# Softmax over the nodes of a graph in a two-layer graph network: from PE transposes for two graphs at a time to a DRAM round trip for one graph at a time

## The chip, the cores and the metric

The kernel runs on one core of a Trainium2 chip. The metric is the device time of one execution in microseconds; lower is better. The time before is 2011.91 us, the median of three runs (2011.75 to 2013.03).

## The reference, cut to what matters

There are 64 graphs (B) of 256 nodes (N) with 512 features (F), all in float32. The node mask is all ones. Two layers follow each other, each with a residual and a layer norm:

```python
# layer 0
deg = sum(adj, -1)
agg = (adj @ x) / max(deg, 1e-6)
x1  = layernorm(x + relu(concat([x, agg]) @ W.T))
# layer 1
q, k = split(x1 @ Wqk); v = x1 @ Wv
agg  = adj @ (k * mask)
w    = mask * sum(q * agg, -1) / sqrt(512)        # one score per node
out  = layernorm(x1 + softmax(w, over the 256 nodes)[:, None] * v)
```

What matters here is the softmax: each graph has 256 scores, one per node, and the softmax runs over all 256. In the kernel a graph's nodes lie on the 128 partitions in two halves, so the scores of one graph are a [128, 2] tile, and the maximum and the sum have to be taken across partitions.

## The kernel before, in words

One loop over i, from 0 to B + G + 1 with G = 2, runs a software pipeline over the graphs. In iteration i the program issues the loads of graph i + 2 (`load`, L78), the dense products of layer 0 for graph i (`layer0_a` L191, `layer0_b` L208), the row sums and the dense products of layer 1 for graph i - 2 (`turn` L286, `layer1_steps` L289), and the product of the adjacency with the values of graph i together with the x1 values of graph i - 1 (`gather_a` L222). After these come the combination and layer norm of layer 0 for graph i (`combine0` L269, `norm0` L277), which ends with the transposition of x1 by VectorE blocks and 16 small DMAs (`transpose_rows` L148, L157), and the degrees and sums for the next graph (`prepare` L173). Layer 1's q and k projections are merged into one matrix ahead of the loop (L110 to L116), so that the score of a node is the dot product of one row with its aggregated row; `dot` (L299) does that on VectorE as the products come out of PSUM.

Every matrix product is done in 2 x 2 blocks with seven block products instead of eight. A bank `u` collects several of them in turn: a product is added to it, ScalarE copies the partial result away (L197, L200, L204, L212 in layer 0; L304, L311, L318 in layer 1; L249, L255, L258, L262 in the gather), and the next product is added on top. TensorE therefore cannot add the next product on `u` before ScalarE's copy of the last is done; products on other banks (p2, p5) lie in between. All dense products are issued at L142, those of the gather at L240. PSUM has eight banks: seven are rotated by `bank()`, one (`ps_tp`) serves the transposes of the softmax.

The softmax works on two graphs at a time. `softmax_rows` (L328) takes the [128, 2, 2] scores of a pair, adds the partial dot and scales by the mask (L330, L331), and transposes them on TensorE (L335) so that each graph is one partition with 256 scores in PSUM. VectorE takes the maximum (L337, L338), ScalarE the exponential with its sum (L341), VectorE divides (L342, L343). `softmax_cols` (L346) transposes the result back on TensorE (L349) and copies it to SBUF (L351). `finish` (L353) multiplies v by the probabilities, adds x1 (L357), normalises (`layer_norm`, L160 to L171, with a square root at L167) and stores the output (L360). The pair's softmax is in the iteration in which i - 4 is even, and a graph is finished four iterations after its layer 0.

The program's text gives the order of dependencies and of priority; the order on each engine is laid out by the framework's planner, which fills all five engines' queues. Each engine then runs its queue strictly in order. SyncE (SP) issues all DMAs of the loop from one queue, so a DMA that waits for its data or buffer holds up those behind it.

Of the kernel before, what the change touches and what calls it, by code (L numbers as in the profile page):

```python
# [31 lines left out]
F32 = mybir.dt.float32  # L35
AF = mybir.ActivationFunctionType
OP = mybir.AluOpType
AX = mybir.AxisListType

P = 128  # L40
Q = 32
G = 2
DEG_EPS = 1e-6
LN_EPS = 1e-5

# [2 lines left out]
def resnorm_kernel(  # L48
# [12 lines left out]
    nc = tc.nc  # L61
    B, N, F = x.shape
    A = wqk_t.shape[0] // 2
    NT, NF, NA = N // P, F // P, A // P
    H, HF = NF // 2, F // 2
    assert NT == 2 and NF == 4
    inv_scale = 1.0 / float(A) ** 0.5

    const = ctx.enter_context(tc.tile_pool(name="const", bufs=1))
    pool = ctx.enter_context(tc.tile_pool(name="pool", bufs=2))  # L70
    small = ctx.enter_context(tc.tile_pool(name="small", bufs=4))
    ps_mm = ctx.enter_context(tc.tile_pool(name="ps_mm", bufs=7, space=bass.MemoryType.PSUM))
    ps_tp = ctx.enter_context(tc.tile_pool(name="ps_tp", bufs=1, space=bass.MemoryType.PSUM))

    (xs, adjs, rows, xTs, sums0, sumsA, rdegs, vals, owns, x1s, x1Ts, sums1, aggs, vs, scores, probs,
     open0) = ({} for _ in range(17))

    def load(g):  # L78
        xTs[g] = pool.tile([P, NF, N], F32, name="xT")
# [12 lines left out]
    with setup as sp:  # L92
# [8 lines left out]
        mask_sb = const.tile([P, NT, B], F32, name="mask_sb")  # L101
# [3 lines left out]
        ident = const.tile([P, P], F32, name="ident")  # L105
# [4 lines left out]
        ps = [ps_mm.tile([P, F], F32, name="mm") for _ in range(NF)]  # L110
# [6 lines left out]
    late = ctx.enter_context(tc.tile_pool(name="late", bufs=2))  # L117
# [22 lines left out]
    def product(ps, a, b, start=True):  # L140
        for c in range(H):
            nc.tensor.matmul(ps, a[:, c, :], b[:, c, :], start=start and c == 0, stop=(c == H - 1),  # L142
                             skip_group_check=True)

    def bank():
        return ps_mm.tile([P, F], F32, name="mm")

    def transpose_rows(src, dst):  # L148


        sq = pool.tile([P, P // Q, NF, NT, Q], F32, name="sq", bufs=1)
        for t in range(NT):
            nc.vector.transpose(sq[:, :, :, t, :].rearrange("p b c q -> p c b q"), src[:, t, :])
        to = dst.rearrange("f c (t a q) -> f (c t) a q", t=NT, q=Q)
        for a in range(P // Q):
            for b in range(P // Q):
                nc.sync.dma_start(to[b * Q:(b + 1) * Q, :, a, :],  # L157
                                  sq[a * Q:(a + 1) * Q, b].rearrange("p c t q -> p (c t) q"))

    def layer_norm(src, dst):  # L160
        mv = small.tile([P, NT, 2], F32, name="mv")
        for t in range(NT):
            st = small.tile([P, 6], F32, name="st")
            nc.vector.bn_stats(st, src[:, t, :])  # L164
            nc.vector.bn_aggr(mv[:, t, :], st)
        rstd = small.tile([P, NT], F32, name="rstd")
        nc.scalar.activation(rstd, mv[:, :, 1], AF.Sqrt, bias=eps)  # L167
        nc.vector.reciprocal(rstd, rstd)
        for t in range(NT):
            nc.vector.tensor_scalar(dst[:, t, :], src[:, t, :], mv[:, t, 0:1], rstd[:, t:t + 1],  # L170
                                    op0=OP.subtract, op1=OP.mult)  # L171
# [44 lines left out]
    def values(g):  # L216

        if g not in vals:
            vals[g] = pool.tile([P, 2, NT, F], F32, name="vals")
        return vals[g]  # L220
# [54 lines left out]
                                           op0=OP.max, op1=OP.add)  # L275

    def norm0(g):  # L277
        x1s[g] = pool.tile([P, NT, F], F32, name="x1", bufs=G + 4)
        layer_norm(owns.pop(g), x1s[g])
        for t in range(NT):  # L280
            nc.scalar.activation(values(g + 1)[:, 1, t, :], x1s[g][:, t, :], AF.Copy,  # L281
                                 scale=mask_sb[:, t, g:g + 1])
        x1Ts[g] = pool.tile([P, NF, N], F32, name="x1T")
        transpose_rows(x1s[g], x1Ts[g])

    def turn(g):  # L286
        sums1[g] = row_sums(x1Ts.pop(g), nc.vector)

    def layer1_steps(g):  # L289
        if g % G == 0:  # L290
            scores[g // G] = (small.tile([P, NT, G], F32, name="scores", bufs=2),
                              small.tile([P, G], F32, name="part", bufs=2))
        sc, part = scores[g // G]
        at = g % G
        s, w, agg = sums1.pop(g), W1, aggs.pop(g + 1)[:, 1]
        v = vs[g] = late.tile([P, NT, F], F32, name="v", bufs=G + 2)
        q = pool.tile([P, F], F32, name="q")

        def dot(a, t, to):  # L299
            nc.vector.scalar_tensor_tensor(q, a, 1.0, agg[:, t, :], op0=OP.mult, op1=OP.mult, accum_out=to)  # L300

        u = bank()
        product(u, s["A11"], w["B11"])
        nc.scalar.copy(q, u)  # L304
        dot(q, 0, part[:, at:at + 1])
        yield
        p5 = bank()
        product(p5, s["S1"], w["T1"])
        yield
        product(u, s["S2"], w["T2"], start=False)  # L310
        nc.scalar.copy(v[:, 0, :], u)  # L311
        yield
        p2 = bank()
        product(p2, s["A12"], w["B21"])
        dot(p2, 0, sc[:, 0, at:at + 1])
        yield
        product(u, s["S3"], w["T3"], start=False)
        nc.scalar.copy(v[:, 1, :], u)  # L318
        nc.vector.tensor_add(v[:, 1, :], p5, v[:, 1, :])  # L319
        yield  # L320
        product(u, s["A22"], w["T4"], start=False)
        dot(u, 1, sc[:, 1, at:at + 1])
        yield
        product(p5, s["S4"], w["B22"], start=False)
        nc.vector.tensor_add(v[:, 0, :], p5, v[:, 0, :])  # L325
        yield

    def softmax_rows(k):  # L328
        w, part = scores.pop(k)
        nc.vector.tensor_add(w[:, 0, :], w[:, 0, :], part)  # L330
        nc.vector.scalar_tensor_tensor(w, w, inv_scale, mask_sb[:, :, k * G:(k + 1) * G],  # L331
                                       op0=OP.mult, op1=OP.mult)
        wr = ps_tp.tile([G, NT, P], F32, name="tp")
        for t in range(NT):
            nc.tensor.transpose(wr[:, t, :], w[:, t, :], ident)  # L335
        top = small.tile([G, 1], F32, name="top")
        nc.vector.reduce_max(top, wr.rearrange("g t p -> g (t p)"), axis=AX.X)  # L337
        nc.vector.tensor_scalar(top, top, -1.0, None, op0=OP.mult)  # L338
        e = small.tile([G, NT, P], F32, name="e", bufs=2)
        total = small.tile([G, 1], F32, name="total")  # L340
        nc.scalar.activation(e, wr, AF.Exp, bias=top, accum_out=total)  # L341
        nc.vector.reciprocal(total, total)  # L342
        nc.vector.tensor_scalar(e, e, total, None, op0=OP.mult)  # L343
        return e

    def softmax_cols(k, e):  # L346
        ps = ps_tp.tile([P, NT, G], F32, name="tp")
        for t in range(NT):
            nc.tensor.transpose(ps[:, t, :], e[:, t, :], ident[:G, :G])  # L349
        probs[k] = small.tile([P, NT, G], F32, name="probs", bufs=2)  # L350
        nc.vector.tensor_copy(probs[k], ps)  # L351

    def finish(g):  # L353
        x1, v, p = x1s.pop(g), vs.pop(g), probs[g // G]
        o = pool.tile([P, NT, F], F32, name="o")
        for t in range(NT):
            nc.vector.scalar_tensor_tensor(o[:, t, :], v[:, t, :], p[:, t, g % G:g % G + 1], x1[:, t, :],  # L357
                                           op0=OP.mult, op1=OP.add)
        layer_norm(o, o)
        nc.sync.dma_start(out[g].rearrange("(t p) f -> p t f", p=P), o)  # L360
# [5 lines left out]
    def step(gen, n=1):  # L366
        for _ in range(n):
            next(gen, None)

    for i in range(B + G + 2):  # L370
        new = i < B
        if i + 2 < B:
            load(i + 2)
        k, at = divmod(i - G - 2, G)
        e = None
        if new:
            layer0_a(i)
        if at == 0 and 0 <= k < B // G:
            e = softmax_rows(k)
        if 0 <= i - 2 < B:  # L380
            turn(i - 2)
        l1 = layer1_steps(i - 2) if 0 <= i - 2 < B else iter(())
        step(l1)
        if new:
            layer0_b(i)
        if e is not None:
            softmax_cols(k, e)
        if 0 <= i - 2 - G < B:
            finish(i - 2 - G)
        z = gather_a(i) if i <= B else iter(())  # L390
        step(l1, 2)
        step(z)
        step(l1)
        step(z)
        step(l1)
        step(z)
        step(l1)
        step(z)
        step(l1)
        step(z)  # L400
        if new:
            combine0(i)
            norm0(i)
        if i + 1 < B:
            prepare(i + 1)
# [26 lines left out]
```

## Time and profile before

| what | value |
|---|---|
| median of three runs | 2011.91 us |
| the profiled execution, its own time | 2011.95 us |
| its span, first to last instruction | 2010.2 us |
| mean granted TensorE clock | 0.994 |
| ScalarE table loads | 32 at L341 (exponential), 33 at L167 (square root), 1 at L177, 1.283 us each |
| transposes on TensorE | 64 at L335 (0.273 us each), 64 at L349 (0.208 us mean) |
| largest single waits of TensorE | 6.2 us for the first weights, 4.1 us for a transposed x1 near the end |
| SyncE: time to landing, medians | x1T 2.0, adj 2.6, rows 2.6, out 3.1, x 3.5, xT 4.1 us |

The profile comes from one execution. Busy time of an engine is the union of the times of its instructions; TensorE's matmuls are pipelined, so the duration of one (0.59 us for 128x512) is longer than the step from one to the next (0.43 us). Each float32 matmul of the listing is two records. Line numbers such as L142 are lines of the kernel's listing; SPq is the queue of SyncE, PEld the weight loads of TensorE. The idle time in a line is the time in which the engine stood still before the instruction, with what ended it.

### The profile page before, as it was taken

The numbers are of one execution on the slowest core, as the hardware profiler recorded it, in microseconds if no ns is written. First come the engines' busy times: TensorE is split into PE (matmuls) and PEld (weight loads), VectorE is DVE, ScalarE is ACT, GpSimd is POOL, SyncE is SP. The second block draws the span as 40 slices with busy tenths as digits, with TensorE's granted clock in tenths as the row PEclk, the third lists the DMA queues.
The fourth block names the chain that finished last, engine by engine and source line by source line (L and its number), as shares of the span: only waits on it lengthen the run. The fifth ranks groups of instructions, "written<-read, shape, count | busy, mean of one in ns | idle before, by whom it ended". The sixth has DMA issues, their size and how long they took to land.

```text
span 2010.2 us, 19340 instructions
## 1 busy us (share of the span) xinstructions
PE 1973.9 (98%) x5536; PEld 1030.4 (51%) x5536; DVE 1523.6 (76%) x3184; ACT 673.2 (33%) x1354; POOL 419.0 (21%) x518
## 2 busy tenths in 40 slices
PE   7999999999999999999999999999999999999995
PEld 3555555555555555555555555555555555555552
DVE  3677787777787777787777887777877777877776
ACT  2333333333333332333332333333333333333322
POOL 4121221221221222212212212212212212222100
PEclk9999999999999999999999999999999999999998
DMA  7333333333333333323333333333333333233211
GB/s 241 85 71 94 88 79 94 86 82 91 88 81 92 90 80 84 99 77 86 90 87 86 80 94 89 79 94 85 81 92 90 81 91 86 68 79 79 62 38 53
DMA packets 384872, 174.40 MB, mean 87 GB/s; under 512 B 283776, under 2 KB 349440, under 8 KB 384768
## 3 DMA queue, kind: packets, MB, share of 16 engines
q1 hardware_dynamic: 382624, 168.97, 32.0%
q10 hardware_dynamic: 2144, 4.19, 0.6%
q8 instruction: 46, 0.75, 0.2%
q14 instruction: 58, 0.48, 0.1%
HBM read 105.97 MB, written 33.55 MB: 69 GB/s over the span
## 4 chain that ended last, share of the span: by engine, by line
PE 95%; DVE 1%; ACT 1%; SPq 0%; issue 0%; DMA 0%; DVEq 0%; ACTq 0%
PE mm L142 75%; PE mm L240 19%; SPq L157 0%; PE tp L349 0%; PE tp L335 0%; DVE st L164 0%; DVE o L357 0%; DVE own L272 0%; ACT L341 0%; ACT vals L281 0%; DMA x1T<-sq 0%; ACT rows L177 0%; DVE o L170 0%; DVE own L274 0%; DVE v L325 0%
## 5 line engine op out<-in xcount | busy, mean ns | idle before, releaser
L142 PE MATMUL mm<-w,s 128*128 128x512 f32 x1024 | 481.3, 592 | 0.7 <-ACT v L311 0.7
L142 PE MATMUL mm<-t,s 128*128 128x512 f32 x1024 | 466.2, 597 | 4.8 <-ACT own L197 3.8
L142 PEld LDWEIGHTS mm<-t,s 128*128 128x128 f32 x1024 | 192.3, 190 | 236.7 <-issue 215.5
L142 PEld LDWEIGHTS mm<-w,s 128*128 128x128 f32 x1024 | 194.4, 190 | 192.8 <-issue 163.2
L142 PE MATMUL mm<-w,x1T 128*128 128x512 f32 x512 | 242.5, 596 | 4.1 <-DMA x1T<-sq 4.1
L142 PE MATMUL mm<-w,xT 128*128 128x512 f32 x512 | 242.0, 594 | 0.0
L183 POOL TENSOR_TENSOR sa<-adj 128x128 f32<-128x128 f32 x64 | 47.1, 736 | 781.0 <-PE mm L240 774.3
L134 POOL TENSOR_TENSOR s<-xT 128x256 f32<-128x256 f32 x64 | 47.7, 745 | 703.6 <-PE mm L142 685.8
L240 PE MATMUL mm<-tv,sa 128*128 128x256 f32 x768 | 187.1, 379 | 0.0
L240 PEld LDWEIGHTS mm<-tv,sa 128*128 128x128 f32 x768 | 145.8, 190 | 74.6 <-issue 59.6
L142 PEld LDWEIGHTS mm<-w,xT 128*128 128x128 f32 x512 | 97.9, 191 | 95.8 <-issue 92.4
L272 DVE SCALAR_TENSOR_TENSOR own<-zr,rdeg,own 128x512 f32<-128x512 f32 x128 | 107.6, 841 | 44.4 <-ACT zr L262 44.4
L319 DVE TENSOR_TENSOR v<-mm,v 128x512 f32<-128x512 f32 x64 | 44.3, 692 | 126.3 <-ACT v L318 126.3
L142 PEld LDWEIGHTS mm<-w,x1T 128*128 128x128 f32 x512 | 95.3, 191 | 86.1 <-issue 74.6
L300 DVE SCALAR_TENSOR_TENSOR q<-mm,zr 128x512 f32<-128x512 f32 x128 | 87.7, 685 | 66.1 <-PE mm L142 66.1
L311 ACT COPY v<-mm 128x512 f32<-128x512 f32 x64 | 37.4, 585 | 299.0 <-PE mm L142 299.0
L142 PE MATMUL mm<-t,x1T 128*128 128x512 f32 x256 | 125.5, 612 | 0.7 <-ACT v L318 0.7
L142 PE MATMUL mm<-t,xT 128*128 128x512 f32 x256 | 120.6, 593 | 3.0 <-ACT vals L204 3.0
L240 PE MATMUL mm<-vals,adj 128*128 128x256 f32 x512 | 121.3, 379 | 1.6 <-DVE vals L214 1.6
L357 DVE SCALAR_TENSOR_TENSOR o<-v,probs,x 128x512 f32<-128x512 f32 x128 | 120.3, 959 | 0.1
L240 PEld LDWEIGHTS mm<-vals,adj 128*128 128x128 f32 x512 | 97.1, 190 | 43.2 <-issue 21.5
L214 DVE TENSOR_TENSOR vals<-mm,vals 128x512 f32<-128x512 f32 x64 | 44.3, 692 | 91.8 <-PE mm L142 91.8
(83 smaller groups left out, 2668.6 us busy)
## 6 DMA issues: line engine op xcount, KB each, us to landing
xT<-x_t SPq DMA_DIRECT2D x64, 512.0 KB, 4.1
x<-x SPq DMA_DIRECT2D x64, 512.0 KB, 3.5
x1T<-sq SPq DMA_DIRECT2D x1024, 32.0 KB, 2.0
out<-o SPq DMA_DIRECT2D x64, 512.0 KB, 3.1
adj<-adj_t SPq DMA_DIRECT2D x64, 256.0 KB, 2.6
rows<-adj SPq DMA_DIRECT2D x64, 256.0 KB, 2.6
wqk<-wqk_t ACTq DMA_DIRECT2D x4, 512.0 KB, 8.6
w<-w_t ACTq DMA_DIRECT2D x2, 1024.0 KB, 11.7
```

Source lines behind the costliest of these rows:

```text
L134: eng.tensor_add(s1, a21, a22)
L142: nc.tensor.matmul(ps, a[:, c, :], b[:, c, :], start=start and c == 0, stop=(c == H - 1), skip_group_check=True)
L183: nc.gpsimd.tensor_add(sa[:, 0], a21, a22)
L214: nc.vector.tensor_add(y[:, 0, :], p5, y[:, 0, :])
L240: nc.tensor.matmul(ps[:, k * HF:(k + 1) * HF], sumsA[g - k][a], w[b][:, n, :], start=start and n == 0, stop=True, skip_group_check=True)
L272: nc.vector.scalar_tensor_tensor(own[:, t, :], z[:, t, :], rdeg[:, t:t + 1], own[:, t, :], op0=OP.mult, op1=OP.add)
L300: nc.vector.scalar_tensor_tensor(q, a, 1.0, agg[:, t, :], op0=OP.mult, op1=OP.mult, accum_out=to)
L311: nc.scalar.copy(v[:, 0, :], u)
L319: nc.vector.tensor_add(v[:, 1, :], p5, v[:, 1, :])
L357: nc.vector.scalar_tensor_tensor(o[:, t, :], v[:, t, :], p[:, t, g % G:g % G + 1], x1[:, t, :], op0=OP.mult, op1=OP.add)
```

## The change

The softmax takes one graph at a time and no longer uses TensorE. `spread` scales the scores as before, stores the [128, 2] tile to a small DRAM tile as a row of 256, and reads this row back so that every partition holds all 256 scores. `softmax` then takes the negated maximum on VectorE and the exponential with its sum on ScalarE on all partitions alike, so that maximum and sum are at once where they are needed; a second exponential makes the graph's own [128, 2] probabilities from the scores still in SBUF. A graph is finished three iterations after its layer 0. `spread` stands at the head of the iteration behind the loads, `softmax` and `finish` in its middle. The bank of the transposes goes to the rotation (eight instead of seven), x1 has five buffers instead of six and v three instead of four.

```diff
-G = 2
...
-    ps_mm = ctx.enter_context(tc.tile_pool(name="ps_mm", bufs=7, space=bass.MemoryType.PSUM))
-    ps_tp = ctx.enter_context(tc.tile_pool(name="ps_tp", bufs=1, space=bass.MemoryType.PSUM))
+    ps_mm = ctx.enter_context(tc.tile_pool(name="ps_mm", bufs=8, space=bass.MemoryType.PSUM))
+    dram = ctx.enter_context(tc.tile_pool(name="dram", bufs=2, space=bass.MemoryType.DRAM))
...
-        x1s[g] = pool.tile([P, NT, F], F32, name="x1", bufs=G + 4)
+        x1s[g] = pool.tile([P, NT, F], F32, name="x1", bufs=5)
...
-        v = vs[g] = late.tile([P, NT, F], F32, name="v", bufs=G + 2)
+        v = vs[g] = late.tile([P, NT, F], F32, name="v", bufs=3)
...
-    def softmax_rows(k):
...
-    def softmax_cols(k, e):
...
+    def spread(g):
+
+        w, part = scores[g]
+        nc.vector.tensor_add(w[:, 0:1], w[:, 0:1], part)
+        nc.vector.scalar_tensor_tensor(w, w, inv_scale, mask_sb[:, :, g], op0=OP.mult, op1=OP.mult)
+        d = dram.tile([NT, P], F32, name="d")
+        nc.sync.dma_start(d.rearrange("t p -> p t"), w, allow_slow_non_contiguous=True)
+        row = rowsW[g] = small.tile([P, N], F32, name="row", bufs=2)
+        nc.sync.dma_start(row, d.rearrange("t p -> (t p)").partition_broadcast(P))
+
+    def softmax(g):
+        (w, _), row = scores.pop(g), rowsW.pop(g)
+        top = small.tile([P, 1], F32, name="top")
+        nc.vector.reduce_max(top, row, axis=AX.X, negate=True)
+        total = small.tile([P, 1], F32, name="total")
+        nc.scalar.activation(row, row, AF.Exp, bias=top, accum_out=total)
+        p = probs[g] = small.tile([P, NT], F32, name="probs", bufs=2)
+        nc.scalar.activation(p, w, AF.Exp, bias=top)
         nc.vector.reciprocal(total, total)
-        nc.vector.tensor_scalar(e, e, total, None, op0=OP.mult)
-        return e
+        nc.vector.tensor_scalar(p, p, total, None, op0=OP.mult)
...
-    for i in range(B + G + 2):
+    for i in range(B + 3):
         new = i < B
         if i + 2 < B:
             load(i + 2)
-        k, at = divmod(i - G - 2, G)
-        e = None
+        if i >= 3:
+            spread(i - 3)
         if new:
             layer0_a(i)
-        if at == 0 and 0 <= k < B // G:
-            e = softmax_rows(k)
...
-        if e is not None:
-            softmax_cols(k, e)
-        if 0 <= i - 2 - G < B:
-            finish(i - 2 - G)
         z = gather_a(i) if i <= B else iter(())
         step(l1, 2)
         step(z)
         step(l1)
         step(z)
-        step(l1)
-        step(z)
-        step(l1)
-        step(z)
-        step(l1)
-        step(z)
+        if i >= 3:
+            softmax(i - 3)
+            finish(i - 3)
+        for _ in range(3):
+            step(l1)
+            step(z)
         if new:
             combine0(i)
             norm0(i)
```

More of the change, by code (lines that the diff above doesn't have):

```diff
@@ L71, in resnorm_kernel @@
     small = ctx.enter_context(tc.tile_pool(name="small", bufs=4))
-    ps_mm = ctx.enter_context(tc.tile_pool(name="ps_mm", bufs=7, space=bass.MemoryType.PSUM))
-    ps_tp = ctx.enter_context(tc.tile_pool(name="ps_tp", bufs=1, space=bass.MemoryType.PSUM))
+    ps_mm = ctx.enter_context(tc.tile_pool(name="ps_mm", bufs=8, space=bass.MemoryType.PSUM))
+    dram = ctx.enter_context(tc.tile_pool(name="dram", bufs=2, space=bass.MemoryType.DRAM))
     (xs, adjs, rows, xTs, sums0, sumsA, rdegs, vals, owns, x1s, x1Ts, sums1, aggs, vs, scores, probs,
-     open0) = ({} for _ in range(17))
+     open0, rowsW) = ({} for _ in range(18))
     def load(g):
@@ L289, in layer1_steps @@
     def layer1_steps(g):
[L290 to L294, printed above, removed]
+        sc, part = scores[g] = (small.tile([P, NT], F32, name="scores", bufs=2),
+                                small.tile([P, 1], F32, name="part", bufs=2))
         s, w, agg = sums1.pop(g), W1, aggs.pop(g + 1)[:, 1]
-        v = vs[g] = late.tile([P, NT, F], F32, name="v", bufs=G + 2)
+        v = vs[g] = late.tile([P, NT, F], F32, name="v", bufs=3)
         q = pool.tile([P, F], F32, name="q")
@@ L304, in layer1_steps @@
         nc.scalar.copy(q, u)
-        dot(q, 0, part[:, at:at + 1])
+        dot(q, 0, part)
         yield
@@ L314, in layer1_steps @@
         product(p2, s["A12"], w["B21"])
-        dot(p2, 0, sc[:, 0, at:at + 1])
+        dot(p2, 0, sc[:, 0:1])
         yield
@@ L321, in layer1_steps @@
         product(u, s["A22"], w["T4"], start=False)
-        dot(u, 1, sc[:, 1, at:at + 1])
+        dot(u, 1, sc[:, 1:2])
         yield
@@ L326, in layer1_steps @@
         yield
-    def softmax_rows(k):
[L329 to L341, printed above, removed]
-        nc.vector.reciprocal(total, total)
-        nc.vector.tensor_scalar(e, e, total, None, op0=OP.mult)
-        return e
@@ L346, in softmax_cols @@
-    def softmax_cols(k, e):
[L347 to L351, printed above, removed]
+    def spread(g):
[6 more added lines that the diff above has]
+        nc.sync.dma_start(row, d.rearrange("t p -> (t p)").partition_broadcast(P))
@@ L353, in finish @@
     def finish(g):
-        x1, v, p = x1s.pop(g), vs.pop(g), probs[g // G]
+        x1, v, p = x1s.pop(g), vs.pop(g), probs.pop(g)
         o = pool.tile([P, NT, F], F32, name="o")
         for t in range(NT):
-            nc.vector.scalar_tensor_tensor(o[:, t, :], v[:, t, :], p[:, t, g % G:g % G + 1], x1[:, t, :],
+            nc.vector.scalar_tensor_tensor(o[:, t, :], v[:, t, :], p[:, t:t + 1], x1[:, t, :],
                                            op0=OP.mult, op1=OP.add)
```

## The prediction

> **What bounds the kernel now.** I read the page's busy shares first, then the busy time by stage, the chain that ended last, and last the timelines of ScalarE and SyncE in one softmax iteration.
>
> ```profile
> PE 1973.9 (98%) x5536; PEld 1030.4 (51%) x5536; DVE 1523.6 (76%) x3184; ACT 673.2 (33%) x1354; POOL 419.0 (21%) x518
> ```
> ```profile
> 98.34:1926.55 1828.21, 1828.21 (x5161) 958.58 (x5161) 1417.12 (x2960) 620.21 (x1235) 390.46 (x480) 1.00 0.32 84
> ```
> The second line is a stage: its length, then busy PE, weight load, DVE, ACT, POOL, the granted clock and DMA share. TensorE is busy for all of 1828.21 us at clock 1.00. Nothing but TensorE work counts there; every other engine counts only if it makes TensorE wait. The chain, in order of time (start, length), shows one period of two graphs:
>
> ```profile
> 1012.45 17.17 PE mm L142 x40
> ...
> 1042.60 8.58 PE mm L142 x20
> 1051.19 0.22 PE tp L335 x2
> 1051.41 5.15 PE mm L142 x12
> 1056.56 0.21 PE tp L349 x2
> 1056.77 3.63 PE mm L142 x8
> ...
> 1073.39 6.87 PE mm L142 x16
> ```
> An iteration without softmax lasts 1042.60 - 1012.45 = 30.15 us, one with it 1073.39 - 1042.60 = 30.79. The transposes and what they disturb cost 0.63 to 0.64 us per pair of graphs: 0.22 + 0.21 for themselves, and 3.63 instead of 8 x 0.43 = 3.44 for the eight records after L349. I use 0.63. This is the whole prize.
>
> ScalarE in that iteration (start, length, instruction, what ended the idle time before):
>
> ```profile
> 1048.51 0.56 ACT L200 COPY vals<-mm 128x512 f32<-128x512 f32 x1
> 1049.42 1.33 ACT L281 ACTIVATE vals<-x,mask_sb 128x512 f32<-128x512 f32 x2
> 1051.22 0.58 ACT L204 COPY vals<-mm 128x512 f32<-128x512 f32 x1 [0.47 <-PE mm L142]
> 1052.68 1.28 ACT L341 ACT_TABLE_LOAD   x1 [0.87 <-DVE top L338]
> 1053.97 0.46 ACT L341 ACTIVATE e<-tp,top 2x256 f32<-2x256 f32 x1
> 1054.44 0.56 ACT L304 COPY q<-mm 128x512 f32<-128x512 f32 x1
> ```
> The softmax now sits where ScalarE has nothing urgent: after the copy L204 and before L304, whose bank TensorE next adds to at about 1058. SyncE:
>
> ```profile
> 1033.25 0.45 SPq L360 DMA_DIRECT2D out<-o  x1
> 1040.06 0.37 SPq L82 DMA_DIRECT2D adj<-adj_t  x1
> 1046.19 0.37 SPq L86 DMA_DIRECT2D x<-x  x1
> 1049.51 0.37 SPq L84 DMA_DIRECT2D rows<-adj  x1
> 1051.08 10.45 SPq L157 DMA_DIRECT2D x1T<-sq  x16
> ```
> Between 1033.7 and 1051.1 it mostly waits for buffers. Note the order: x goes out before rows, unlike the listing. The planner seems to order each queue by when it takes work to be ready, so an instruction's place in the listing is not its place in time.
>
> **What the Trainium skill says.** "ScalarE: Activation LUTs", What ACT_TABLE_LOAD costs: 1283 ns for any set, plus about 1380 ns of drain; the trace has 1.283 us at L341 and L167 and the Exp starting 1.29 after it, so I use 1.283. The same page, Table sets, puts exp and sqrt in different sets: the trace has 32 loads for Exp and 33 for Sqrt. "DMA: Bandwidth & Descriptors", Anatomy of one DMA: about 2.0 us fixed, mostly the receipt of the write, worse to HBM; the trace has 2.0 for x1T (into SBUF) and 3.1 for out (into DRAM). The same page, Rules for kernel authors: a strided last dimension is one descriptor per element, so the column store is 256 pieces of 4 bytes; no row of before shows that, though x1T also has 256 pieces (32 x 8, 128 bytes).
>
> **The change, part by part.**
> - Transposes out (L335, L349, 64 each). 30 of the 32 pairs lie in the saturated stage: 30 x 0.63 = **-18.9 us**. The other two lie in the tail.
> - VectorE. Out, per pair: 0.161 + 0.162 + 0.394 + 0.131 + 0.150 + 0.341 + 0.152 (L330, L331, L337, L338, L342, L343, L351) = 1.49, or 0.75 a graph. In, per graph: add and scale 0.32, reduce_max over 256 0.39 (L337 has the same length; upper end 0.42 from L134's 128x256), reciprocal 0.15, scale 0.15: 1.01. So +0.26 x 64 = 17 us in 486 idle. Cost nothing if it fits the gaps; DVE was busy 24.76 of 30.78 us in the softmax iteration.
> - ScalarE. Out, per pair: 1.283 + 0.465 + 0.185, and one Sqrt load: 3.2. In, per graph: Exp load, row Exp 0.465 + 0.185 (same length as L341), column Exp about 0.29 (as L167's 128x2), Sqrt load: 3.5. ACT goes from 673 to about 673 + 64 x 1.9 = 794 us, 40%. No cost as a sum. As a block in the queue, Exp load to column Exp is 2.2 us: it is free between L204 and L304; elsewhere not (rival 1).
> - Two DMAs on SyncE. The column store waits for scores (ready at 1040.1, right after the last dot, as L331 now) and lands in 2.0 to 3.1 us; the row read waits for that and is 128 KB, 2.0 (x1T, 32 KB) to 2.6 (adj, 256 KB). The round trip is 4 to 5.7, I take 4.8; rows can be there at 1045. Queued behind the waiting read are x, rows, x1T and out. They already wait until 1046 to 1051, so 0 is taken; if the two go out late instead, x1T is delayed by up to 4 us, against 9 us before its reader (x1T issued until 1061.5, landed 2.0 later, read at 1073.5).
> - Finish one graph per iteration, an iteration earlier and behind two gather steps: same instructions (o 2 x 0.959 the dearest), its out DMA now behind the row read. 0; vals and tv, which TensorE needs, no longer queue behind o at 1057.9, which gains nothing as TensorE did not wait there.
> - Banks 7 to 8: the saturated stage has no wait on a bank: 0. x1 6 to 5 and v 4 to 3: a graph holds v from its layer 1 to finish in the next iteration, so two live; x1 about three: 0.
> - Tail. Before, the last scores are ready at 1993.57 and VectorE ends at 2006.25, with two graphs finished there. After: store and read 4.8 (1998.4), reduce 0.4, Exp load 1.28, Exps 0.8, two small DVE steps 0.35 (2001.3), o 1.42, statistics 1.5, rstd and reciprocal 0.5, normalise 1.0: 2005.7, **-0.6** (range -2 to +2). Ahead of it, the last x1T is late by a Sqrt load (1960.91, just after the pair's Exp) that its rstd met: 1.3 may go or stay; and x1T then waits 4.11 us on DMA anyway. I take **-1.0** of 0 to -2; the pair's own 0.4 of transposes is hidden by that wait.
>
> Sum: -18.9 - 0.6 - 1.0 = -20.5, on the profiled run of 2011.95 (span 2010.2, 1.75 around it; the median of the runs shown is 2011.91): **1991.5 us**, a span of 1989.7.
>
> **Rivals.**
> 1. A block on ScalarE in front of a copy that TensorE waits for (slower). Without transposes nothing holds the softmax back to 1051: with rows at 1045, reduce_max can slip into VectorE's gap at 1048.0 to 1048.6 and the Exp block into ScalarE at 1050.75, ahead of L204. That copy then starts near 1053.0 instead of 1051.2; the next product on its bank is due at 1052.75. Wait: 1053.0 + 0.58 - 1052.75 = 0.8; from 0.45 (column Exp behind the copy) to 1.2 (an iteration like the one at 1012, where L204 ends at 1021.81 against 1022.59 and the whole 2.0 falls ahead). If rows come late, the program's own place is as bad: near 1035 the copy L318 has no slack (TensorE waits 0.05 to 0.08 on it already). It decides from 0.63 / 2 = 0.31 us an iteration. At 0.8 x 62 = +50: **2041 us** (2019 to 2066). For it: the tail shows this wait twice, 0.59 on L304 behind an Exp load and 0.68 on L311. Against: 30 Exp blocks and 30 Sqrt loads now make no wait at all.
> 2. A small recurring wait of 0.1 to 0.3, from a Sqrt load for finish, now every iteration, or from VectorE held in order for Exp (now 1.96 us per pair, harmless): 0.2 x 62 = +12.4: **2004 us**.
> 3. The row comes late: SyncE puts the read behind the 16 x1T DMAs (10.5 us), rows land near 1065, VectorE stands at reduce_max with combine and norm behind it. Those have 9 us of slack; beyond it, about 0.5 us an iteration: **2022 us**, from 2004. Against: SyncE idles when scores are ready.
>
> That the change does not do what it says can hardly be: the instructions leave TensorE.
>
> **How the numbers follow.** Forecast 0.50 (its own range 1987 to 1997), rival 1 0.26, rival 2 0.14, rival 3 0.10. A measurement can tell about 0.2% from no change, 4 us. Faster: 0.50 + 0.08 of rival 2 = 0.58; same: 0.06 + 0.04 of rival 3 = 0.10; slower: 0.26 + 0.06 = 0.32. The range is 1986 to 2040: below, the bounds of the tail; above, it leaves out half of rival 1 and the ends of the others, under 2 in 10.
>
> **What would show it.** Right: pieces of the chain 30.15 apart in every iteration, PE busy for all of that stage with no L335 or L349, Exp blocks between L204 and L304. Rival 1: waits of L142 on ACT copies, about 60 times, behind an Exp or Sqrt load. Rival 3: long waits of VectorE for the row DMA. I am wrong if TensorE has recurring idle over 0.3 us an iteration, or if the iteration is 30.15 and the tail is over 5 us longer.

## The result, and the profile after

The kernel after the change takes 2554.47 us, the median of four runs (2551.04 to 2564.02), against 2012.47 us before (four runs, 2011.75 to 2013.19). The ratio is 1.2701, with a 95% interval of 1.2666 to 1.2736: 27% slower, where 1% faster was forecast. The profiled execution took 2564.02 us, its span is 2562.2 us, and the mean granted TensorE clock is 0.907 (0.994 before).

From the page of the kernel after: its busy shares, TensorE and its clock in 40 slices of the span, the chain that ended last by engine, and two groups whose last columns are the idle time before them and what ended it.

```profile
PE 2121.3 (83%) x5408; PEld 1067.2 (42%) x5408; DVE 1559.6 (61%) x3280; ACT 950.6 (37%) x1668; POOL 417.8 (16%) x518
...
PE   7979888888797888798888987978878878888884
...
PEclk9999898898898898998998989989989899898896
...
PE 51%; DMA 33%; ACT 9%; DVE 2%; issue 2%; SPq 1%; ACTq 0%; DVEq 0%
...
L340 ACT ACT_TABLE_LOAD x64 | 82.1, 1283 | 607.3 <-DVE top L338 583.2
...
L338 DVE TENSOR_REDUCE top<-row 128x1 f32<-128x256 f32 x64 | 26.9, 420 | 398.8 <-DMA row<-d 398.8
```

TensorE has lost 128 transposes and is yet busy for 147 us more. It is idle for 2562.2 - 2121.3 = 440.9 us, against 36.3 before, spread over the whole span and not in one place. The chain, which was TensorE's own work before (95% of it), now holds DMA for a third. The waits of the kernel after (us in total, times, longest) name the links, and the page gives the median times to landing (last number) of the store and the read:

```profile
ACT L340 <- DVE top L338: 583.2, 61, 18.8
PEld mm L142 <- ACT vals L200: 433.8, 62, 8.2
DVE top L338 <- DMA row<-d: 398.8, 64, 11.3
PE mm L142 <- ACT vals L200: 383.0, 61, 7.4
...
d<-scores SPq DMA_DIRECT2D x64, 1.0 KB, 8.2
row<-d SPq DMA_DIRECT2D x64, 128.0 KB, 5.1
```

About 61 times, once per iteration, TensorE waits for ScalarE's copy L200, ScalarE for the maximum L338, and VectorE for the row. The copy L200 belongs to layer 0 and needs nothing of the softmax. One iteration of the chain that ended last (start, length):

```profile
1031.94 8.02 DMA d<-scores
...
1039.98 5.16 DMA row<-d
...
1045.16 0.43 DVE top L338
...
1045.64 1.28 ACT L340
...
1047.56 1.28 ACT L167
...
1048.85 0.29 ACT rstd L167
1049.15 0.48 ACT vals L200
...
1049.67 9.73 PE mm L142 x18
1059.40 1.92 PE mm L240 x8
...
1070.50 8.70 DMA d<-scores
```

The store of the scores lands after 8.0 us and the read after 5.2. Maximum, table load and Exp follow, then the load and the square root of a layer norm, and only then the copy L200 that releases TensorE. The next scores exist 20.4 us after TensorE starts again (at 1070.07), and 0.4 later, behind the issue of an adj load, the store starts again: a closed loop of 38.56 us (40.04 for the one before it) where an iteration of TensorE's work is 30.15. ScalarE's timeline shows that this is an order of its queue; in the listing L200 comes ahead of `softmax`:

```profile
1006.09 1.28 ACT L340 ACT_TABLE_LOAD   x1 [9.76 <-DVE top L338]
1007.39 0.51 ACT L340 ACTIVATE row<-row,top 128x256 f32<-128x256 f32 x1
...
1008.00 1.28 ACT L167 ACT_TABLE_LOAD   x1
1009.30 0.30 ACT L167 ACTIVATE rstd<-mv,eps 128x2 f32<-128x2 f32 x1
1009.50 0.57 ACT L200 COPY vals<-mm 128x512 f32<-128x512 f32 x1
...
1011.80 1.28 ACT L342 ACT_TABLE_LOAD   x1
```

The planner has put the maximum and the first Exp at the start of the iteration, though the row comes later; the second Exp (L342) falls behind a square root, so there are up to four table loads per graph, 251 at the three lines (64 at L340, 126 at L167, 61 at L342), instead of 65 before. TensorE at the same place:

```profile
1002.41 1.02 PE L142 MATMUL mm<-t,s 128*128 128x512 f32 x2
1010.12 3.78 PE L142 MATMUL mm<-w,s 128*128 128x512 f32 x4 [6.69 <-ACT vals L200]
1013.70 2.86 PE L142 MATMUL mm<-t,s 128*128 128x512 f32 x4
1016.39 1.88 PE L142 MATMUL mm<-t,xT 128*128 128x512 f32 x4
```

It stands for 6.69 us, and the four records after that take 3.78 us instead of 1.88. The granted clock of 1003.3 to 1010.1, 1010.1 to 1017 and 1017 to 1031 is 0.91, 0.60 and 1.00. The Trainium skill, "TensorE: Matmul & The Clock Gate", Part 1: The HAM clock gate, says that the array falls to half its clock after an idle window of some 3.4 us and comes back after about as long a busy one. The trace's record of the clock agrees in the main: after has 65 stretches of half clock, 63 of them 3.4 us or two or three times that, and every stop over 3.6 us brings one. Below that the length of the stop does not decide: in experiment 1 the four records took 1.98 us after a stop of 2.92, and 3.56 after one of 2.35.

### The profile page after: what moved, and what is told of

Read it like the earlier page. It is cut to its first block, busy times and chain, and to the rows that moved or that the text cites. A ratio compares the mean times of both kernels' runs of the same rounds, so it can differ in the third digit from the quotient of the medians.

```text
span 2562.2 us, 19599 instructions
## 1 busy us (share of the span) xinstructions
PE 2121.3 (83%) x5408; PEld 1067.2 (42%) x5408; DVE 1559.6 (61%) x3280; ACT 950.6 (37%) x1668; POOL 417.8 (16%) x518
## 4 chain that ended last, share of the span: by engine, by line
PE 51%; DMA 33%; ACT 9%; DVE 2%; issue 2%; SPq 1%; ACTq 0%; DVEq 0%
PE mm L142 38%; DMA d<-scores 21%; PE mm L240 13%; DMA row<-d 12%; ACT L340 3%; ACT L167 3%; ACT vals L200 1%; DVE top L338 1%; SPq L82 1%; ACT rstd L167 1%; ACT row L340 1%; DVE q L297 0%; ACT vals L281 0%; DMA adj<-adj_t 0%; DVE st L164 0%
## 5 line engine op out<-in xcount | busy, mean ns | idle before, releaser
L142 PE MATMUL mm<-w,s 128*128 128x512 f32 x1024 | 595.9, 712 | 392.1 <-ACT vals L200 383.0
L142 PE MATMUL mm<-t,s 128*128 128x512 f32 x1024 | 512.5, 626 | 3.7 <-ACT own L197 3.2
L142 PEld LDWEIGHTS mm<-w,s 128*128 128x128 f32 x1024 | 220.6, 223 | 640.9 <-ACT vals L200 433.8
L142 PEld LDWEIGHTS mm<-t,s 128*128 128x128 f32 x1024 | 216.2, 211 | 295.3 <-issue 264.9
L338 DVE TENSOR_REDUCE top<-row 128x1 f32<-128x256 f32 x64 | 26.9, 420 | 398.8 <-DMA row<-d 398.8
L240 PE MATMUL mm<-vals,adj 128*128 128x256 f32 x512 | 128.7, 394 | 10.8 <-ACT vals L281 9.2
L255 ACT COPY zr<-mm 128x512 f32<-128x512 f32 (+1 forms) x65 | 37.7, 580 | 233.6 <-PE mm L240 233.6
L197 ACT COPY own<-mm 128x512 f32<-128x512 f32 x64 | 37.5, 586 | 227.1 <-PE mm L142 227.1
```

What stands on the lines that cost most here:

```text
L197: nc.scalar.copy(own[:, 0, :], u)
L240: nc.tensor.matmul(ps[:, k * HF:(k + 1) * HF], sumsA[g - k][a], w[b][:, n, :], start=start and n == 0, stop=True, skip_group_check=True)
L255: nc.scalar.copy(r12, of(u))
L338: nc.vector.reduce_max(top, row, axis=AX.X, negate=True)
```

## The experiments

The theory, formed from the trace of after: the loop above, made of two parts. The consumers of the row stand in order ahead of L200 in two queues, and the round trip is 13.3 us (the sum of the medians 8.2 and 5.1), not 4.8. Rival A: it is ScalarE's block of table loads in front of L200. Rival B: the two DMAs on SyncE delay the loads behind them. Kernels of which one run was made have one time; the runs of before on the same chips had medians of 2011.78 to 2012.15 us.

**1. The read does not depend on the store.** The store stays, but the row that the maximum and the sum are taken from is a row of x; the order on TensorE and ScalarE stays that of after, but for a few records at the end:

```diff
-        nc.sync.dma_start(row, d.rearrange("t p -> (t p)").partition_broadcast(P))
+        nc.vector.tensor_copy(row[:, 0:NT], w)
+        nc.sync.dma_start(row, x[g, 0, 0:N].partition_broadcast(P))
```

> The changed kernel, but the row read takes 256 values of x instead of the stored scores and waits only for the scores (a tiny copy into row), not for the store, which still goes out. It leaves the scores out of the maximum and the sum. The order on every engine is that of the changed kernel. Theory (the store's 8.2 us lie in a loop scores - store - read - maximum - Exp - rstd - copy L200 - products - scores): the loop shrinks from 39 to about 30.8 us, near TensorE's own 30.15, TensorE's long waits on L200 vanish, the half clock with them: 2010 to 2100 us. Rival A (the three table loads per iteration in front of urgent copies are the cause, the DMA is not): all loads stay, so over 2300 us. Rival B (SyncE's queue is late for x1T and the loads): the store no longer holds the queue, so it falls too, to about 2000 to 2100.

Measured: 2337.23 us. The theory's number missed, and rival A's (over 2300) fits. But the read did not become as short as was meant, so this run does not decide between them; experiments 7 and 11 do. From the chain of this kernel, and its page (the last number is the median time to landing):

```profile
1019.30 9.41 DMA row<-x
...
1054.38 11.57 DMA row<-x
```
```profile
row<-x SPq DMA_DIRECT2D x64, 128.0 KB, 9.3
```

The read no longer waits, and lands 9.3 us after its issue, when the store in front of it lands too (9.5). The Trainium skill, "DMA: Bandwidth & Descriptors", Queues, rings and completion order, says that the write of a DMA's semaphore lands only after every earlier write of that DMA engine; the trace agrees: the last piece of the read is moved 3.1 us after its issue (median), 6.2 before it is reported as landed, and without the store the same read lands in 3.0 (experiment 11). From ready scores to the landed row it is 10.2 us here, where the store is issued first, and 13.7 in after (medians). TensorE's wait on L200 falls from 383.0 to 200.3 us in all, and the time falls with it.

**2. The DMAs beside the kernel before.** Both DMAs for each graph of a pair, and nobody reads the row:

```diff
+        for h in range(G):
+            d = dram.tile([NT, P], F32, name="d")
+            nc.sync.dma_start(d.rearrange("t p -> p t"), w[:, :, h], allow_slow_non_contiguous=True)
+            row = small.tile([P, N], F32, name="row", bufs=2)
+            nc.sync.dma_start(row, d.rearrange("t p -> (t p)").partition_broadcast(P))
```

> The kernel before with the change's two DMAs per graph added (store of the scores, row read waiting for it, both on SyncE), with nobody reading the row. Theory (only the waiting of VectorE and ScalarE for the row costs): 2010 to 2030 us, the store again about 8 us to landing. Rival B (SyncE held by the store's wait makes x1T and loads late): over 2100 us. Rival A says nothing new: no table loads are added, about 2012.

Measured: 2013.86 us. SyncE's own waits in this kernel (here L338 issues the read of the row, L83 loads adj) show the same slow store, and it harms no one:

```profile
SPq L83 <- PE mm L241: 311.5, 60, 8.0
SPq L338 <- DMA d<-scores: 238.3, 44, 8.8
```

The medians to landing are 8.2 and 5.4 us as in the kernel after. Rival B falls: the transfers as such cost about nothing here, nor in experiments 4 and 9, and what hurts is that somebody waits for the row.

**3. No table exchanges.** The layer norms leave out their square root (Identity in its place), and no load is needed for it any more:

```diff
-        nc.scalar.activation(rstd, mv[:, :, 1], AF.Sqrt, bias=eps)
+        nc.scalar.activation(rstd, mv[:, :, 1], AF.Identity, bias=eps)
```

> The changed kernel with Identity in place of Sqrt in the layer norms (the root is left out of the computation), so that no Exp or Sqrt table has to be exchanged; the order on the engines stays. Theory (DMA in the loop): two loads of 1.28 leave a loop of 39 us, 36.3 to 36.5 us per iteration, 2330 to 2400 us. Rival A (table loads are the cause): below 2100 us. Rival B (SyncE's queue): no change, about 2550.

Measured: 2554.48 us, the time of after, though ScalarE is busy for 619.4 us instead of 950.6. Rival A falls as the main cause. The theory's number missed too; rival B's (about 2550) fits, but experiment 2 speaks against B, and the chain shows why this is no clean comparison with after:

```profile
1032.93 8.47 DMA d<-scores
...
1041.42 5.30 DMA row<-d
...
1046.75 0.42 DVE top L338
...
1048.04 0.48 ACT vals L200
...
1048.56 13.37 PE mm L142 x24
```

The planner has laid TensorE's queue out anew: 24 records stand behind L200 before the gather instead of 18, so six more are held up by the row. Experiment 10, which has this order too, shows what the store costs in it.

**4. The consumers later in the queues.** The maximum and both Exps are held in program order, and `softmax` and `finish` come after the first of the three last pairs of steps, near the end of the iteration:

```diff
-        nc.vector.reduce_max(top, row, axis=AX.X, negate=True)
+        tc.keep_in_program_order(nc.vector.reduce_max(top, row, axis=AX.X, negate=True))
...
+        step(l1)
+        step(z)
         if i >= 3:
             softmax(i - 3)
             finish(i - 3)
-        for _ in range(3):
+        for _ in range(2):
```

(and likewise for the two Exps).

> The changed kernel with the maximum and both Exps pinned in the program's order and emitted one gather step later, behind the ScalarE copies L315 and L258: about 20 us after the store instead of 8. All DMAs, all waits of SyncE and Exp and Sqrt loads in every iteration stay. Theory (an in-order wait for a round trip of 13 us, placed too early): the row is there when it is asked for, TensorE stays busy, 1990 to 2030 us. Rival A (table loads): over 2200. Rival B (SyncE's queue): over 2400.

Measured: 2003.6 us (2001.08 to 2004.3), a ratio of 0.9953 to before (0.9937 to 0.997). Busy shares and the chain:

```profile
PE 1954.0 (98%) x5408; PEld 1023.6 (51%) x5408; DVE 1527.2 (76%) x3280; ACT 792.2 (40%) x1546; POOL 349.0 (17%) x518
```
```profile
1004.40 17.17 PE mm L142 x40
...
1034.56 17.17 PE mm L142 x40
```

The same instructions (table loads apart), with the same slow round trip (8.4 and 5.2 us), take 551 us less. The iteration is 30.16 us, there are no recurring waits of TensorE, and 129 table loads instead of 251 at the three lines (64 at L340, 65 at L167): both Exps now stand side by side. What is left is at the end, where two graphs' round trips lie one behind the other on the chain (10.85 and 3.62, then 8.50 and 4.87 us).

**5. What a store of 1 KB costs, by its form.** In the kernel before, one DMA per pair of graphs, in turn in five forms, for which nobody waits (`src` holds the scores in its first columns, `d4` and `d8` are DRAM tiles):

```diff
+        if form == 0:
+            nc.sync.dma_start(d4.rearrange("t p -> p t"), src[:, 0:NT], allow_slow_non_contiguous=True)
+        elif form == 1:
+            nc.sync.dma_start(d8, src[:, 0:NT])
...
```

> The kernel before with one DMA more per pair, that nobody waits for, in five forms in turn: d4 the change's store (256 pieces of 4 bytes into 1 KB), d8 the same bytes in 128 pieces of 8 bytes, d64 128 pieces of 64 bytes, far 256 pieces of 4 bytes each 512 bytes apart, rowx a read of one row of x onto all partitions with no store near it. The stored values are of no use to the result. The time stays about 2012. If the 8 us of the store are paid per piece, d8 and d64 land in about 4 to 5 us and far in 8; if they come from small pieces that share lines of the memory, d64 and far land in 2 to 3; if they are the price of any store to DRAM, all four take 8, which out's 3.1 us speaks against. rowx in 2.0 to 2.6 if the read itself is cheap, about 5 if a row read 128 times over is slow by itself.

Measured, us to landing (2018.67 us for the whole; the 7 us over the kernel before arise in the first 70 us, and the steady stage is as long as there):

| form | n | min | median | max |
|---|---|---|---|---|
| 256 pieces of 4 bytes into one row of 1 KB, as in the change | 7 | 8.6 | 9.2 | 9.8 |
| 128 pieces of 8 bytes into 1 KB | 7 | 3.0 | 4.2 | 5.3 |
| 128 pieces of 64 bytes into 8 KB | 6 | 2.4 | 2.5 | 2.6 |
| 256 pieces of 4 bytes, 512 bytes apart | 6 | 1.5 | 2.5 | 2.6 |
| read of a row of x onto 128 partitions | 6 | 3.3 | 4.2 | 4.4 |

Neither the number of pieces nor DRAM as such makes the store slow: as many pieces, as small, land in 2.5 us when they lie apart. What costs is small pieces that lie together. Sending them does not take the time: in all four stores the trace has the last piece moved 1.0 to 2.2 us after the issue, and the difference lies between that and the report of the landing.

**6. Held in program order, at the listing's own place.** Only the pins of experiment 4:

```diff
-        nc.scalar.activation(row, row, AF.Exp, bias=top, accum_out=total)
+        tc.keep_in_program_order(nc.scalar.activation(row, row, AF.Exp, bias=top, accum_out=total))
```

(and likewise for the maximum and the second Exp).

> As the run that moved the softmax one gather step later, but left at the listing's own place: maximum and both Exps pinned there, so the Exp block (load 1.28, Exps and read 0.9) comes before the copy L315, on which TensorE already waits 0.05 to 0.08 us per iteration. Theory (a block in front of a copy without slack costs its length past the time when the copy falls due): the block ends 1.1 us after the copy was due, 62 x 1.1 = +68, so 2050 to 2090 us, with TensorE waiting for L315. If the round trip alone decides, as it is over by then, about 2004 as in the moved version.

Measured: 2033.96 us, better than expected. The recurring wait on the copies of layer 1 that was feared did not come; the iteration is 30.54 us, and its loss runs through VectorE to the copy L204.

```profile
1006.78 1.28 ACT L340
...
1037.32 1.28 ACT L340
```

For the main question this is the purest run: the edit takes away nothing but the planner's freedom to move three instructions, and 520 of the 542 us between the medians of before and after go.

**7. The after kernel with a store of 8 bytes a partition.** The row then has its nodes in another order, which a maximum and a sum do not see:

```diff
-        d = dram.tile([NT, P], F32, name="d")
-        nc.sync.dma_start(d.rearrange("t p -> p t"), w, allow_slow_non_contiguous=True)
+        d = dram.tile([P, NT], F32, name="d")
+        nc.sync.dma_start(d, w)
...
-        nc.sync.dma_start(row, d.rearrange("t p -> (t p)").partition_broadcast(P))
+        nc.sync.dma_start(row, d.rearrange("p t -> (p t)").partition_broadcast(P))
```

> The changed kernel with the scores stored in the order of the partitions, 128 pieces of 8 bytes in place of 256 of 4; maximum and sum do not depend on the order. Theory (the store lies in the loop): each microsecond that the store is shorter takes 64 us and some half-clock time off. If the price is per piece, 4 to 5 us less, 2250 to 2330 us; if not, about 2550.

Measured: 2161.07 us, with all five engines in the same order as in after: the form of the store alone is worth 393 us. Waits of this kernel:

```profile
PE mm L142 <- ACT vals L200: 99.6, 59, 3.2
DVE top L338 <- DMA row<-d: 98.8, 61, 6.1
```

Store and read land in 4.1 and 4.5 us. The time falls below the forecast, because not only the wait shrinks: the stretches of half clock fall from 476.8 us in after to 62.7. At a wait of 0.89 us the four records after it take 1.98 us.

**8. Experiment 4 with the last two graphs together.** `softmax` and `finish` of the last two graphs come in the last iteration, to let their round trips overlap:

```diff
+        for g in {B + 1: (), B + 2: (B - 2, B - 1)}.get(i, (i - 3,)):
+            if g >= 0:
+                softmax(g)
+                finish(g)
```

> The version with the softmax one gather step later, and in the tail the softmax of graph 62 is emitted behind the last scores, so that VectorE does not wait for graph 62's row ahead of graph 63's last dot products, and the two round trips lie beside each other. Theory: the steady stage stays at 30.15 us per iteration, and the tail loses one of two round trips in series (10 us of 1961 to 1990): 1990 to 1996 us, ratio 0.989 to 0.992. If the tail is bound by something else, about 2003.

Measured: 2003.36 us (2002.31 to 2004.27), 0.9959 (0.9945 to 0.9972); the theory's number missed, and the other case named (about 2003) came. The end is set by when the last x1T lands. After it comes the last layer 1, with the last scores at 1977.65 us, and one round trip still stands between them and the end: 24.9 us from scores to the end of the span, where before needed 16.6 (1993.57 to 2010.2).

**9. Experiment 8 with the store of experiment 7.**

> The version with the softmax later and the tail's two graphs together, with the store in 128 pieces of 8 bytes. In the steady stage nothing waits for the round trip, so 30.15 us per iteration as before; in the tail one round trip lies on the path, and the store is 4.1 instead of 8.4 us, the read 4.5 instead of 5.2. Theory: 5 us less than 2003.4, 1996 to 2000 us, ratio 0.992 to 0.994. If the tail is bound elsewhere, about 2003.

Measured: 1996.94 us (1994.57 to 1998.09), 0.9927 (0.9913 to 0.9941), the fastest version here; it beats both kernels. TensorE is busy for 98% of its span, as before.

**10. Experiment 7 without table exchanges.** The edit of experiment 3 on top of experiment 7.

> The changed kernel with the 8-byte store and with Identity in place of Sqrt (the root is left out), so that no table is exchanged; its order on every engine is that of the run without the Sqrt table. Theory (the round trip first, the blocks on ScalarE behind it second): against that run's 2554 the store gives 4 to 5 us an iteration and most of the half clock, and against the 2161 of the 8-byte store alone the table loads now show, because they lie behind a shorter round trip: 2015 to 2080 us. Rival A (table loads first): as the loads gave nothing with the slow store, it can't say why they should now.

Measured: 2126.36 us; the forecast missed. As in experiment 3, 24 records stand behind L200, and the loop is 31.9 us long (the next store starts at 1042.83). Its chain:

```profile
1010.97 3.91 DMA d<-scores
...
1014.89 4.63 DMA row<-d
...
1020.84 0.48 ACT vals L200
...
1021.36 10.57 PE mm L142 x24
```

Experiments 3 and 10 have the same order on every engine and differ in the store alone: 428 us. Experiments 7 and 10 differ by the loads and by the six records at once, so the 35 us between them (0.6 an iteration) are not the price of the loads alone.

**11. Experiment 1 without the store.** Nothing is stored, and the row is a row of x:

```diff
-        d = dram.tile([NT, P], F32, name="d")
-        nc.sync.dma_start(d.rearrange("t p -> p t"), w, allow_slow_non_contiguous=True)
```

> As the first run (row read from x, waiting only for the scores), but with no store at all: what the change would cost if its round trip were a single read of about 4.5 us, close to the 4.8 us of the forecast. The scores are left out of the maximum and the sum. The order on PE and ScalarE is that of the changed kernel, with its three table loads per iteration in front of the same copies. Theory (the length of the round trip is the mis-sized term, and the read of the first run was held up by the store beside it): the row is there at 5 us after the scores, before VectorE comes to the maximum; ScalarE's block ends about when TensorE needs the copy L200, 1990 to 2030 us. Rival A (the blocks with table loads in front of L200 and L204 cost by themselves): 0.5 to 1.2 us an iteration remain, 2025 to 2070. If the read takes 9 to 11 us without a store too: about 2340 as in the first run.

Measured: 2048.65 us (2046.96 to 2049.34), 1.0178 (1.0161 to 1.0195). The row lands in 3.0 us and VectorE waits for it three times in all. The chain now runs through VectorE, which comes late to the maximum, and ScalarE:

```profile
1013.90 4.56 PE mm L142 x10
...
1037.18 1.28 ACT L339
...
1039.09 1.28 ACT L167
...
1040.68 0.47 ACT vals L200
...
1042.89 1.28 ACT L341
...
1044.48 0.48 ACT vals L204
...
1045.00 4.56 PE mm L142 x10
```

The last piece shown starts 31.10 us after the first, 0.95 more than in experiments 4 and 9. Rival A was right here, and the theory's number missed: with a row that lands even sooner after the scores (3.5 us, median) than the 4.8 us of the forecast, the order that the planner chose still ends slower than before.

## Why the prediction was wrong

**The budget.** The span grew by 2562.2 - 2010.2 = 552 us. TensorE's idle time is 404.6 of it (440.9 - 36.3). The other 147.4 are busy time, nearly all of it from the half clock: TensorE is busy for 290.9 of the 476.8 us of half clock, and as the same work takes about half as long at full clock, some 145 us of this are extra (an estimate; about 5 in the kernel before).

**The prize: right.** Experiments 4 and 9 have 30.15 to 30.16 us in every iteration, the forecast's number, with no transposes.

**"The round trip is 4 to 5.7, I take 4.8": the step that failed first.** It is 13.3 us. The store was taken at 2.0 to 3.1 us, from rows of transfers of 32 and 512 KB; its 256 pieces of 4 bytes take 8.2. The prediction named those pieces and said that no row of before shows them, and then took the price of other rows all the same. (The 2.0 us fixed that it cites beside them holds, by the heading of the section, for DMAs issued from GpSimd; these are issued from SyncE.) The read was taken at 2.0 to 2.6 and takes 5.1. With TensorE's and ScalarE's queues as in after (but for the end), and the row landed 3.6, 9.0, 10.7 and 13.7 us after the scores are ready (means), the time is 2049, 2161, 2337 and 2554 us (experiments 11, 7 and 1, and after). From 9.0 to 10.7 and on to 13.7 the sum comes out: the longer trip, 62 times, and the estimated half clock give 184 and 230 us, where the spans differ by 176 and 227.

**"As a block in the queue ... free between L204 and L304": the order.** The forecast assumed this place; rival 1 saw that nothing holds the block there. Its kind of wait is what experiment 11 measures: 0.95 us an iteration and 2048.65, for 0.8 and 2041. That the sizes lie so near is partly luck, since there the block stands ahead of L200 as well as L204, with up to four loads, and VectorE is late too. With the real round trip the same order has another price, since the queues that stand at the row hold L200 too. That needs both parts: with the pins alone the time is 2034, with the short trip alone 2049 (experiments 6 and 11), and with both faults together 2554. That the planner takes the row to be ready sooner than it is, is argued from where it put the block, not shown; its own figures were not seen.

**Rival 3: the right victim and the wrong cause.** VectorE does stand at the maximum for the row (398.8 us), with other work behind it. But SyncE issues the read at once when the store lands, not behind the x1T transfers, and the price of 0.5 us an iteration had not seen that the loop closes: the copy behind the row is needed for the next scores, so the wait returns each iteration.

**ScalarE: "No cost as a sum": right in the sum, wrong in its parts.** Forecast 794 us with two loads per graph: 792 in experiments 4 and 9. In after the second Exp has a load of its own, and a second square root another, hence 951. The loads are not the main cost: with the store as in after, leaving them out gains nothing (experiment 3), and what they cost alone was not separated from the order.

**The half clock: not priced.** It is worth about 140 of the 552 us. No wait of that length recurs in the kernel before, and none was forecast.

**VectorE, DMAs beside, banks and buffers at 0: right** as far as experiments 2, 4 and 9 show: no recurring wait there.

**The tail: -0.6 forecast, +1.6 at best.** In experiment 9 the last scores are ready at 1974.62, 18.95 us earlier than before, and the end follows 18.2 us after them instead of 16.6. There the last row lands at 1981.75, 7.1 us after the scores, where 4.8 were taken, and its maximum starts at once (1981.79). VectorE is done with the graph before it at about the same time, so a shorter trip alone would not have helped. So even the best version has a span of 1992.8 us, where the forecast had 1989.7.

## What to carry to other kernels

Price a transfer by its form as well as by its bytes, and when no row shows the form, keep the range open at the long end and ask what happens there. Before giving the consumer of a DMA to a planner, look at what will be queued behind it on its engine, and whether that leads back to the DMA's own input; such a loop brings the wait back in every iteration. The cure was to hold the consumer behind the work that it had held up (520 us), to move it on to where the data are surely there (551 in all), and only then to shorten the transfer (another 6.4, in experiment 9 against 8).

## What the runs showed of the hardware that was not expected

- A store of 256 pieces of 4 bytes into one row of 1 KB of DRAM lands in 8.2 to 9.5 us (medians by kernel); 128 pieces of 8 bytes into the same 1 KB in 4.0 to 4.2; 256 pieces of 4 bytes that lie 512 bytes apart in 2.5. The pieces are moved within 2.2 us in every form of experiment 5; the rest passes before the landing is reported. Why that is long for small pieces that lie together was not tried further and stays open.
- A read issued right behind such a store in the same queue lands in 9.3 us instead of 3.0, though it needs nothing of it and its own pieces are moved within 3.1. Other transfers grow beside it too: x takes 6.0 us in after and 3.5 before.
- One row of 1 KB onto all partitions takes 3.0 to 5.4 us, more than a load of twice the bytes from a plain layout (2.6).
- TensorE works at about half its speed after every stop over 3.6 us in these traces (3.78 us for four records after 6.69, instead of 1.88), for 3.4 us or a multiple of it by the clock's record. Between some 2 and 3.6 us some stops bring it and some do not: 3.56 us for four records after a stop of 2.35, but 1.98 after one of 2.92 (both in experiment 1).
